# Layer 3 of a four-layer graph network: attention-weight tiles taken in pairs, their products as one run of 64 records

## The chip, the core and the metric

The kernel runs on one core of a Trainium2 chip. The metric is the device time of one execution in microseconds (us), the median of several runs. The core's engines work side by side and meet only at semaphores: TensorE (PE; its weight loads are shown as PEld), VectorE (DVE), ScalarE (ACT), GpSimd (POOL) and SyncE (SP), which here only issues transfers. PE writes its products to PSUM, a small memory of banks of 512 float32 a partition; everything else lives in SBUF.

## The reference: what is computed

Sixteen graphs of 1024 nodes with 256 features pass through four layers; each layer normalises its input (layer norm, then ReLU) and adds its output to it. Layers 0, 1 and 3 are attention layers, layer 2 is a mean over neighbours. Of layer 3, with 4 heads of 64 features, what matters is this:

```python
h = jnp.einsum('bnd,hde->bhne', nodes_embed, W)
e_src = jnp.einsum('bhne,hte->bhtn', h, a_src)
e_dst = jnp.einsum('bhne,hte->bhtn', h, a_dst)
# adjacency is 0 or 1 here, so one edge type is present
weight = mask * (e_src[:, :, 0, :, None] + e_dst[:, :, 0, None, :])
weight = jax.nn.leaky_relu(weight, negative_slope=0.01)
weight = jnp.where(node_adj[:, None] == 0, NEG, weight)
attention = jax.nn.softmax(weight, axis=-1)
dst = jnp.einsum('bhij,bhje->bhie', attention, h) + bias[None, :, None, :]
out = jax.nn.relu(dst) + h          # then a layer norm over the 64 features
```

The exponential of a leaky ReLU of a sum is a maximum of two products, so a tile of unnormalised weights can be made by one DVE instruction from a broadcast row, a column and the mask. The sum of each row of weights comes out of the same product as the result, from a column of its own beside the 64 features: 65 columns a head.

## The kernel before

The sixteen graphs are generators which a small queue steps in turn: a graph starts 120 units of planned time after the one before it, so that about two graphs are under way and one's layer 3 lies beside the next one's layers 0 and 1. The numbers after `yield` are planned time and decide the order in which the program is recorded; a scheduler then fixes the order of each engine. On the chip each engine runs its own list strictly in that order.

The pools that matter: one PSUM pool for layer 3 and layer 2 (`hd_ps`, 2 banks), and three buffers of 128x1024 float32 for the weight tiles of layer 3 (`p3`).

```python
NT, HALF, PER = N // P, 512, 4          # 8 tiles of 128 nodes, 4 of them a PSUM bank
HO, HW = 64, 65
...
hd_ps = ctx.enter_context(tc.tile_pool(name="hd_ps", bufs=2, space=bass.MemoryType.PSUM))
...
def project(norm, w, n, width):         # L659
    ps = mm_ps.tile([P, HALF], F32, tag="mm", name="ps_proj")
    for c in range(DC):
        nc.tensor.matmul(ps[:, :width], norm.ht[:, c, n * P : (n + 1) * P], w[:, c, :width], ...)
    return ps
```

Layer 1 of the next graph, which runs at the same time. The first two output tiles are summed while the weight tiles are still being made, the other six afterwards:

```python
def layer1(b, xs, mask, norm, after):
    ...
    for j in range(NT):
        nc.scalar.activation(hs[:, j, :D], hs[:, j, :D], AF.Copy, scale=hs[:, j, D : D + 1])
        p = weights("p1")                                                    # 8 buffers
        nc.vector.scalar_tensor_tensor(p, row, q[:, j : j + 1], mask[:, j, :], op0=OP.max, op1=OP.mult)  # L793
        ps_.append(p)
        for i, ps in enumerate(early):                                       # two output tiles
            product(ps, i, j)                                                # L786, 128x257
        yield 1.3
    for i in range(NT):
        ...                                                                  # six more, 8 products each
        nc.vector.reciprocal(z, ps[:, D : D + 1])                            # L807
        ...
        residual(xs, i, v, after, e)                                         # L707, L708; then L627
        yield 3.9
```

Layer 3:

```python
def layer3(b, xs, mask, norm, res):
    ...
    yield 8
    for h in range(H):
        next_row = everywhere(d_row[h + 1], "row3") if h + 1 < H else None
        pss = [hd_ps.tile([P, HALF], F32, tag="hd", name="ps_o3") for _ in range(NHALF)]
        for j in range(NT):
            p = work.tile([P, N], F32, tag="p3", name="p3", bufs=3)
            nc.vector.scalar_tensor_tensor(p, row, q[:, j, h : h + 1], mask[:, j, :], op0=OP.max, op1=OP.mult)  # L887

            for i in range(NT):
                g, k = divmod(i, PER)
                for c in range(2):
                    part = slice(c * P // 2, (c + 1) * P // 2)
                    nc.tensor.matmul(                                        # L893
                        pss[g][part, k * HW : (k + 1) * HW], p[:, i * P : (i + 1) * P][:, part], hbv[:, j, h, :],
                        start=(j == 0 and k == 0), stop=(j == NT - 1 and k == PER - 1), skip_group_check=True,
                    )
            yield 1.4
        for g in range(NHALF):
            o = pss[g][:, : PER * HW].rearrange("p (k e) -> p k e", e=HW)
            rz = small.tile([P, PER], F32, tag="rz", name="rz")
            nc.vector.reciprocal(rz, o[:, :, HO])                            # L901
            nc.vector.tensor_tensor(res[:, g * PER : (g + 1) * PER, h, :], o[:, :, :HO], ..., op=OP.mult)  # L902
        row = next_row
    return hs
```

The products of layer 3 use half of the array's columns each: `part` is a slice of 64 columns of weights, so the two products `c = 0` and `c = 1` lie in different halves of the array and write different halves of the partitions. Every float32 product leaves two records in the trace, so a weight tile (8 row tiles x 2 halves) makes 32 records at L893, and a 128-column product of L659 or L786 makes two.

Of the kernel before, what the change touches and what calls it, by code (L numbers as in the profile page):

```python
# [8 lines left out]
F32 = mybir.dt.float32  # L9
U8 = mybir.dt.uint8  # L10
AF = mybir.ActivationFunctionType
OP = mybir.AluOpType
AX = mybir.AxisListType

P = 128
# [406 lines left out]
def tile_simple_stack(  # L422
# [11 lines left out]
    nc = tc.nc  # L434
    B, N, D = x.shape
    NT = N // P
# [5 lines left out]
    PER = NT // NHALF  # L442
# [4 lines left out]
    HW = HO + 1  # L447
# [20 lines left out]
    work = ctx.enter_context(tc.tile_pool(name="work", bufs=2))  # L468
# [187 lines left out]
# [3 lines that stand above are left out]
            nc.tensor.matmul(ps[:, :width], norm.ht[:, c, n * P : (n + 1) * P], w[:, c, :width], start=(c == 0), stop=(c == DC - 1))  # L659
        return ps  # L660

    def new_hs(name="hs"):
        return state.tile([P, NT, W3], F32, tag="hs", name=name, bufs=4)

    def spread(col, n, scales, name):

        k = n * NT  # L670
        ps = tr_ps.tile([P, P], F32, tag="tr", name="ps_col")
        nc.tensor.transpose(ps[:k, :], col, ident)
        all_rows = []
        for scale in scales:
            e = small.tile([H * NT, P], F32, tag="e_row", name="e_row", bufs=2)
            nc.scalar.activation(e[:k, :], ps[:k, :], AF.Exp, scale=scale)
            d = dram.tile([n, N], F32, tag=f"row_{name}", name="d_row", bufs=4)
            later(nc.sync.dma_start(d.rearrange("r (t p) -> (r t) p", p=P), e[:k, :]))
            all_rows += [d[r] for r in range(n)]
        return all_rows  # L680

    def everywhere(d, tag):
        row = work.tile([P, N], F32, tag=tag, name="row", bufs=2)
        later(nc.sync.dma_start(row, d.partition_broadcast(P)))
        return row

    def column(src, n):

        col = small.tile([P, H, NT], F32, tag="col", name="col", bufs=2)
        nc.vector.tensor_copy(col[:, :n, :], src.rearrange("p t n -> p n t"))  # L690
        return col[:, :n, :].rearrange("p n t -> p (n t)")

    def watch(b, layer, terms):
        k = b * 3 + layer
        nc.vector.tensor_reduce(top[:, k : k + 1], terms, axis=AX.XY, op=OP.max, apply_absolute_value=True)
# [163 lines left out]
    def layer3(b, xs, mask, norm, res):  # L859
        hs = new_hs()  # L860
        terms = hs[:, :, D:]
        hb = new_hs("hb")
        hbv = hb[:, :, : H * HW].rearrange("p t (h e) -> p t h e", e=HW)
        for n in range(NT):
            ps = project(norm, wx[3], n, W3)
            nc.scalar.activation(hs[:, n, :], ps[:, :W3], AF.Copy, scale=norm.rs[n])
            if n % 2:
                pair = slice(n - 1, n + 1)
                nc.scalar.activation(hbv[:, pair, :, HO], terms[:, pair, H:], AF.Exp, scale=S3)
                t = hbv[:, pair, :, :HO]  # L870
                hv = hs[:, pair, :D].rearrange("p t (h e) -> p t h e", e=HO)
                bias = rows["bias3"].rearrange("p (h e) -> p h e", e=HO).unsqueeze(1).to_broadcast([P, 2, H, HO])
                nc.vector.tensor_tensor(t, hv, bias, op=OP.add)
                nc.vector.tensor_tensor(t, t, hbv[:, pair, :, HO:].to_broadcast([P, 2, H, HO]), op=OP.mult)
            yield 1.2
        d_row = spread(column(terms[:, :, :H], H), H, (S3 - 1.0,), "l3")
        row = everywhere(d_row[0], "row3")
        watch(b, 2, terms)
        q = small.tile([P, NT, H], F32, tag="q3", name="q3", bufs=2)
        nc.scalar.activation(q, terms[:, :, H:], AF.Exp, scale=1.0 - S3)  # L880
        yield 8
        for h in range(H):
            next_row = everywhere(d_row[h + 1], "row3") if h + 1 < H else None
            pss = [hd_ps.tile([P, HALF], F32, tag="hd", name="ps_o3") for _ in range(NHALF)]
            for j in range(NT):
                p = work.tile([P, N], F32, tag="p3", name="p3", bufs=3)
                nc.vector.scalar_tensor_tensor(p, row, q[:, j, h : h + 1], mask[:, j, :], op0=OP.max, op1=OP.mult)  # L887

                for i in range(NT):
                    g, k = divmod(i, PER)  # L890
                    for c in range(2):
                        part = slice(c * P // 2, (c + 1) * P // 2)
                        nc.tensor.matmul(  # L893
                            pss[g][part, k * HW : (k + 1) * HW], p[:, i * P : (i + 1) * P][:, part], hbv[:, j, h, :],
                            start=(j == 0 and k == 0), stop=(j == NT - 1 and k == PER - 1), skip_group_check=True,
                        )
                yield 1.4
            for g in range(NHALF):
                o = pss[g][:, : PER * HW].rearrange("p (k e) -> p k e", e=HW)
                rz = small.tile([P, PER], F32, tag="rz", name="rz")  # L900
                nc.vector.reciprocal(rz, o[:, :, HO])  # L901
                nc.vector.tensor_tensor(  # L902
                    res[:, g * PER : (g + 1) * PER, h, :], o[:, :, :HO], rz.unsqueeze(2).to_broadcast([P, PER, HO]), op=OP.mult
                )
            row = next_row
        return hs
# [42 lines left out]
    def graph(b):  # L949
        xs = loaded.pop(b)  # L950
        m = masks.pop(b)
        norm = Norm()
        for g in range(NT // 2):
            norm.pair(xs, g)
            m.step()
            yield 2
        for layer, inputs in ((layer0, (m,)), (layer1, (m.bytes,)), (layer2, ())):
            yield 2
            norm.flip()
            after = Norm()  # L960
            yield from layer(b, xs, *inputs, norm, after)
            norm = after
        yield 2
        norm.flip()
        res = state.tile([P, NT, H, HO], F32, tag="res", name="res", bufs=1)
        hs = yield from layer3(b, xs, m.bytes, norm, res)
        return tail(b, xs, hs, res)
# [25 lines left out]
    while queue:  # L993
        queue.sort(key=lambda g: g[:2])
        at, b, g = queue.pop(0)
# [8 lines left out]
    t = work.tile([P, D], F32, tag="e", name="t_bad")[:, : B * NT]  # L1004
# [77 lines left out]
```

## Time and profile before

| | |
|---|---|
| time, median of 3 runs (lowest, highest) | 2709.49 us (2709.22, 2711.38) |
| profiled execution, span | 2701.4 us |
| granted TensorE clock, mean | 0.978 |
| ACT busy | 1432.5 us, 53% |
| PEld busy | 2018.0 us, 75% |
| DMA, mean rate | 87 GB/s |
| seventh graph's layer 3, first weight tile to the next graph's first weight tile | 1205.95 us to 1369.23 us |
| the last graph's layer 3, first weight tile to the last product's start | 2630.14 us to 2673.1 us |

A matmul is recorded with its whole latency, although the next one starts long before it has ended. So a busy PE is not a PE at its peak, and the time a product costs in a stream is the distance between the starts of neighbouring records, not the mean duration. "Idle before" counts only the time in which no record of that engine was open. A wait is put down to the instruction whose semaphore came last. Line numbers are those of the kernel before.

### The profile page before, as it was taken

How to read it: one execution, taken by the hardware profiler on the slowest of the kernel's cores; microseconds unless marked ns; L12 is line 12 of the kernel's file. 1: busy time of each engine (PE TensorE's matmuls, PEld its weight loads, DVE VectorE, ACT ScalarE, POOL GpSimd, SP SyncE). 2: the span in 40 equal slices, each digit the busy share in tenths (PEclk: the TensorE clock that was granted, in tenths of full speed). 3: DMA queues.
4: the chain of work that ended last, by engine and by line, in shares of the span. 5: the costliest groups of instructions: out<-in, count | busy, mean ns of one | idle time of the engine just before them, and what ended most of it. 6: DMA issues, size and time to landing. Idle time of an engine off the chain costs nothing.

```text
span 2701.4 us, 62281 instructions
## 1 busy us (share of the span) xinstructions
PE 2504.5 (93%) x25682; PEld 2018.0 (75%) x25682; DVE 2021.2 (75%) x4069; ACT 1432.5 (53%) x4065; POOL 418.1 (15%) x390
## 2 busy tenths in 40 slices
PE   5899999999999999999999999999999999999985
PEld 4677787776777778687776877778787777877764
DVE  4357768687686977779677687887778777786868
ACT  4663755627455364654637546374653737546250
POOL 1010212102121030211102111020210202121021
PEclk7899999999999999999999999999999999999998
DMA  4431322424223242331413224242332413224121
GB/s 145 117 83 52 114 72 67 122 64 125 76 69 108 65 120 66 98 80 64 133 53 114 72 64 125 65 133 68 96 82 64 133 52 114 74 63 113 37 63 35
DMA packets 146073, 233.73 MB, mean 87 GB/s; under 512 B 9392, under 2 KB 94512, under 8 KB 145776
## 3 DMA queue, kind: packets, MB, share of 16 engines
q1 hardware_dynamic: 74608, 145.73, 16.7%
q0 software_dynamic: 71168, 83.89, 12.4%
q8 instruction: 205, 3.36, 0.5%
q14 instruction: 92, 0.75, 0.1%
HBM read 212.35 MB, written 17.24 MB: 85 GB/s over the span
## 4 chain that ended last, share of the span: by engine, by line
PE 50%; DMA 13%; issue 13%; DVE 13%; ACT 10%; POOL 1%; SPq 0%; DVEq 0%; POOLq 0%; ACTq 0%
PE ps_o L893 14%; PE ps_o L730 12%; PE ps_proj L659 9%; PE ps_o L786 9%; DMA raw<-in_adj_t 5%; PE ps_o L844 5%; DVE p L887 4%; DMA adj<-in_adj 4%; DMA row<-d_row 3%; PE pt_h L653 2%; ACT hn L631 2%; ACT mask L575 2%; ACT unread L635 1%; DMA d_row<-e_row 1%; DVE p L793 1%
## 5 line engine op out<-in xcount | busy, mean ns | idle before, releaser
L887 DVE SCALAR_TENSOR_TENSOR p<-row,q,mask 128x1024 f32<-128x1024 f32 x512 | 635.3, 1276 | 38.8 <-PE ps_o L893 30.0
L659 PE MATMUL ps_proj<-wx,ht 128*128 128x258 f32 (+2 forms) x2048 | 631.5, 444 | 19.4 <-ACT hs L717 12.8
L893 PEld LDWEIGHTS ps_o<-hb,p 128*64 128x64 f32 x16384 | 513.2, 139 | 126.1 <-issue 72.2
L893 PE MATMUL ps_o<-hb,p 128*64 128x65 f32 x16384 | 563.1, 225 | 16.2 <-DVE p L887 11.1
L786 PE MATMUL ps_o<-hs,p 128*128 128x257 f32 x2048 | 529.7, 398 | 50.0 <-DVE p L793 41.0
L730 PE MATMUL ps_o<-hs,p 128*128 128x256 f32 x2048 | 492.6, 387 | 14.5 <-ACT hs L744 14.0
L659 PEld LDWEIGHTS ps_proj<-wx,ht 128*128 128x128 f32 x2048 | 362.2, 190 | 186.7 <-issue 75.5
L786 PEld LDWEIGHTS ps_o<-hs,p 128*128 128x128 f32 x2048 | 372.1, 193 | 112.6 <-issue 48.5
L730 PEld LDWEIGHTS ps_o<-hs,p 128*128 128x128 f32 x2048 | 383.8, 193 | 70.7 <-ACT hs L744 15.3
L592 POOL TENSOR_SCALAR rs<-mv 128x4 f32<-128x4 f32 (+1 forms) x112 | 56.9, 508 | 1600.3 <-ACT unread L635 1584.7
L631 ACT ACTIVATE hn<-xs,shift 128x256 f32<-128x256 f32 x512 | 236.1, 501 | 115.7 <-DVE shift L627 112.9
L707 DVE SCALAR_TENSOR_TENSOR xs<-e,xs 128x256 f32<-128x256 f32 x256 | 108.2, 423 | 236.8 <-ACT e L762 204.3
L593 POOL TENSOR_TENSOR rs<-rs,neg_half 128x4 f32<-128x4 f32 (+2 forms) x144 | 259.7, 1806 | 10.7
L809 ACT ACTIVATE e<-ps_o,shares 128x256 f32<-128x256 f32 x128 | 59.7, 466 | 349.7 <-DVE shares L807 345.5
L575 ACT ACTIVATE mask<-raw 128x512 uint8<-128x512 int32 x256 | 160.5, 630 | 133.8 <-DMA raw<-in_adj_t 114.7
L844 PE MATMUL ps_o<-hi,adj 128*128 128x258 f32 x1024 | 184.9, 308 | 35.5 <-ACT hi L832 23.7
L653 PE MATMUL pt_h<-ident,hn 128*128 128x128 f32 x1024 | 177.5, 283 | 16.5 <-ACT hn L631 16.2
L635 ACT ACTIVATE unread<-xs,shift 128x256 bf16<-128x256 f32 x384 | 190.7, 497 | 0.6
L844 PEld LDWEIGHTS ps_o<-hi,adj 128*128 128x128 f32 x1024 | 144.3, 192 | 60.7 <-ACT hi L832 29.7
L740 DVE SCALAR_TENSOR_TENSOR p<-row,q 128x1024 f32<-128x1024 f32 x128 | 161.1, 1269 | 30.5 <-DMA row<-d_row 30.5
L654 ACT COPY ht<-pt_h 128x512 f32<-128x512 f32 x256 | 147.2, 588 | 67.3 <-PE pt_h L653 66.8
L708 DVE SCALAR_TENSOR_TENSOR xs<-v,xs 128x256 f32<-128x256 f32 x384 | 161.6, 421 | 26.2 <-ACT v L764 9.7
(101 smaller groups left out, 2644.4 us busy)
## 6 DMA issues: line engine op xcount, KB each, us to landing
raw<-in_adj_t SPq DMA_DIRECT2D x256, 256.0 KB
adj<-in_adj POOLq DMA_DIRECT2D x64, 1024.0 KB, 5.8
row<-d_row SPq DMA_DIRECT2D x112, 512.0 KB
xs<-in_x POOLq DMA_DIRECT2D x32, 512.0 KB, 6.3
out<-res SPq DMA_DIRECT2D x32, 512.0 KB
wx<-in_w SPq DMA_DIRECT2D x3, 256.0 KB
d_row<-e_row SPq DMA_DIRECT2D x48, 4.0 KB
wts<-in_w_t SPq DMA_DIRECT2D x2, 256.0 KB
```

Of the source, the lines that this page charges most:

```text
L575: nc.scalar.activation(self.bytes[:, n, g * HALF : (g + 1) * HALF], raw, AF.Square, accum_out=squares[:, k : k + 1])
L593: nc.gpsimd.tensor_tensor(rs[:, :n], rs[:, :n], neg_half[:, :n], op=OP.pow)
L631: nc.scalar.activation(hn, xs[:, 2 * g + k, :], AF.Relu, bias=shift[:, k : k + 1])
L635: nc.scalar.activation(unread, xs[:, 2 * g + k, :], AF.Square, bias=shift[:, k : k + 1], accum_out=self.var[:, 2 * g + k : 2 * g + k + 1])
L653: nc.tensor.transpose(pt[:, c, k * P : (k + 1) * P], hn[:, c * P : (c + 1) * P], ident)
L659: nc.tensor.matmul(ps[:, :width], norm.ht[:, c, n * P : (n + 1) * P], w[:, c, :width], start=(c == 0), stop=(c == DC - 1))
L708: nc.vector.scalar_tensor_tensor(x, v, 0.0, x, op0=OP.max, op1=OP.add, accum_out=after.sums[:, i % 2 : i % 2 + 1])
L730: m = nc.tensor.matmul(ps[:, :D], ps_[j][:, i * P : (i + 1) * P], hs[:, j, :D], start=(j == 0), stop=(j == NT - 1))
L786: nc.tensor.matmul(ps[:, : D + 1], ps_[j][:, i * P : (i + 1) * P], hs[:, j, : D + 1], start=(j == 0), stop=(j == NT - 1))
L844: nc.tensor.matmul(ps[:, : D + 2], adj_n[g][:, i, jj : jj + P], h[:, i, : D + 2], start=(h is hi and i == 0), stop=(h is lo and i == NT - 1),)
L887: nc.vector.scalar_tensor_tensor(p, row, q[:, j, h : h + 1], mask[:, j, :], op0=OP.max, op1=OP.mult)
L893: nc.tensor.matmul(pss[g][part, k * HW : (k + 1) * HW], p[:, i * P : (i + 1) * P][:, part], hbv[:, j, h, :], start=(j == 0 and k == 0), st ...
```

## The change

Layer 3's weight tiles are given out in pairs. The two DVE instructions of a pair come first, then all 32 products of the pair (64 records) as one block. The block starts with the second tile: its products of row tile 0 and row tile 4, one for each bank. So PE waits for the later of the two tiles at the start of the block, and nothing in the block waits for a tile. Then come all products of the first tile, and then the rest of the second. The flags that clear a bank move to the product that is now the first in it. The pool stays at three buffers. The planned time of a step doubles with its content. The purpose is to go less often between products of 64 columns and products of 128 columns.

```diff
-            for j in range(NT):
-                p = work.tile([P, N], F32, tag="p3", name="p3", bufs=3)
-                nc.vector.scalar_tensor_tensor(p, row, q[:, j, h : h + 1], mask[:, j, :], op0=OP.max, op1=OP.mult)
-
-                for i in range(NT):
+            for j in range(0, NT, 2):
+                ps_ = []
+                for jj in range(j, j + 2):
+                    p = work.tile([P, N], F32, tag="p3", name="p3", bufs=3)
+                    nc.vector.scalar_tensor_tensor(p, row, q[:, jj, h : h + 1], mask[:, jj, :], op0=OP.max, op1=OP.mult)
+                    ps_.append(p)
+
+
+                runs = [(1, 0), (1, PER)] + [(0, i) for i in range(NT)] + [(1, i) for i in range(NT) if i % PER]
+                for t, i in runs:
                     g, k = divmod(i, PER)
                     for c in range(2):
                         part = slice(c * P // 2, (c + 1) * P // 2)
                         nc.tensor.matmul(
-                            pss[g][part, k * HW : (k + 1) * HW], p[:, i * P : (i + 1) * P][:, part], hbv[:, j, h, :],
-                            start=(j == 0 and k == 0), stop=(j == NT - 1 and k == PER - 1), skip_group_check=True,
+                            pss[g][part, k * HW : (k + 1) * HW], ps_[t][:, i * P : (i + 1) * P][:, part], hbv[:, j + t, h, :],
+                            start=(j == 0 and t == 1 and k == 0), stop=(j == NT - 2 and t == 1 and k == PER - 1),
+                            skip_group_check=True,
                         )
-                yield 1.4
+                yield 2.8
```

## The prediction

> **What bounds the kernel now.** I read the page's table of engines first, then its groups, then the chain of waits and the timeline of one graph's layer 3. The page:
>
> ```profile
> PE 2504.5 (93%) x25682; PEld 2018.0 (75%) x25682; DVE 2021.2 (75%) x4069; ACT 1432.5 (53%) x4065; POOL 418.1 (15%) x390
> ...
> L887 DVE SCALAR_TENSOR_TENSOR p<-row,q,mask 128x1024 f32<-128x1024 f32 x512 | 635.3, 1276 | 38.8 <-PE ps_o L893 30.0
> ...
> L893 PE MATMUL ps_o<-hb,p 128*64 128x65 f32 x16384 | 563.1, 225 | 16.2 <-DVE p L887 11.1
> L786 PE MATMUL ps_o<-hs,p 128*128 128x257 f32 x2048 | 529.7, 398 | 50.0 <-DVE p L793 41.0
> ```
>
> PE is the bound of the whole, but 93% and 75% are means over stages. The busy time by stretches of the seventh graph (columns: stretch, its length, then PE, PEld, DVE, ACT, POOL) shows which stage the change touches:
>
> ```profile
> 1205.90:1231.00 25.10, 24.33 (x544) 20.43 (x542) 22.74 (x27) 9.84 (x26) 3.18 (x2) 1.00 0.17 56
> 1231.00:1268.00 37.00, 34.77 (x583) 28.14 (x584) 34.48 (x61) 9.13 (x26) 0.00 (x0) 1.00 0.17 57
> 1268.00:1369.00 101.00, 96.02 (x477) 76.69 (x477) 68.45 (x166) 69.46 (x203) 23.78 (x22) 0.98 0.37 107
> ```
>
> In the 62 us that hold layer 3, DVE is busy for 22.74 of 25.1 us and 34.48 of 37: it has as little room as PE. In the 101 us after it, PE is the bound (96.02) and DVE is not. So a gain on PE in layer 3 may be taken by DVE, and a delay there isn't won back later.
>
> What a change between the two kinds of product costs is not an idle time in any view; it stands in the distances of pieces in the chain of waits (start, length, piece):
>
> ```profile
> 1238.68 1.06 PE ps_o L786 x4
> 1239.74 1.08 PE ps_o L893 x32
> 1240.82 1.93 PE ps_o L786 x8
> ...
> 1256.59 2.02 PE ps_o L893 x64
> 1258.60 0.63 PE ps_o L786 x2
> ```
>
> Eight records of 128 columns take 1.93, four take 1.06: 0.217 each, so a visit of four has 0.19 over. 64 records of 64 columns take 2.02, 32 take 1.08: 0.0294 each, so a run has 0.14 over. In the records the three places are plain and alike everywhere: 310 ns instead of 217 before the first record of a run, 152 ns after its last (instead of 52), and 321 instead of 217 between the first two records after it. A round trip costs about 0.32 us.
>
> **What the Trainium skill says.** "TensorEngine Tiling (Array Packing)", section Key Properties: "Changing tiling mode (not just tile) drains the TensorE". Products of 64 columns are column tiles, those of L786 and L659 are not; the 0.32 us is that drain, and the trace agrees that it falls at each change and at no other place. "TensorE: Matmul & The Clock Gate", section Part 3, says that tiles of different columns compute concurrently; the trace agrees: records of a pair start 8 ns apart, and the pairs 60 ns apart. The page gives no price for the drain. I found nothing on the depth of a buffer ring that bears on three buffers taken by twos.
>
> **The change, part by part.** No instruction is added or removed: 512 DVE tiles, 16384 records. The order of PE in the built program changes from 331 runs of 64-column records to 211 (a last run of 1024 is in both). So 120 round trips go, 8 for each of the first 15 graphs: 120 x 0.32 = 38 us of PE, if PE set the time everywhere.
>
> Against it stands the ring of three buffers. Call the tiles of pair k a(k) and b(k), and R(k) the start of its run. Tile n takes the buffer of tile n-3: a(k) that of b(k-2), b(k) that of a(k-1). In the run the last record of a is the 40th, so it starts at R+1.18 (39 x 0.030). Before, DVE started a tile 0.29 after the start of the last record that reads its buffer (1222.56, where the sixteenth record after 1221.82 started at about 1222.27). So b(k) starts no earlier than R(k-1)+1.45; it takes 1.28, and PE starts 0.06 after that (1207.29 after 1205.95+1.28). With nothing else to do, two runs are at least 1.45+1.34 = 2.79 apart, while PE needs 64 x 0.0294 = 1.88 and DVE 2 x 1.20 (8 tiles in 9.64). In the old order the loop was open: three tiles ahead, and DVE ran at 1.20 a tile where PE had room.
>
> I walk the seventh graph in the new order, with these durations, the order of DVE as built, and everything before 1205.95 unchanged. R1 = 1208.84 (b ready; 18 records of L659 stand ahead of it, where 10 did). R2 = 1211.95, R3 = 1215.04, R4 = 1218.13: here PE's own list decides (2.02 + 1.07 for a projection), and DVE waits 0.7 a pair. R5 is the next head: its banks come free when DVE, busy with b(5) until 1220.8, has done the two divisions; 1221.55, PE waits 0.3. Then three runs with only a small transpose between them, each bound by the ring: R6 = 1224.49, R7 = 1227.28, R8 = 1230.07, waits 0.7, 0.9, 0.9. Next L786's first tiles: the old order had DVE make two more layer 3 tiles ahead of them, and PE waited 2.5:
>
> ```profile
> 1225.73 4.89 PE L893 MATMUL ps_o<-hb,p 128*64 128x65 f32 x160
> 1233.14 2.30 PE L786 MATMUL ps_o<-hs,p 128*128 128x257 f32 x8 [2.52 <-DVE p L793]
> ```
>
> In the new order they come right after b(8), at 1229.93, so this wait goes. But it only moves: DVE then has 2 tiles for L793, two divisions and a(9), b(9) in one chain, so R9 = 1235.8 after a wait of 1.6. From here to R12 DVE is busy without a break, and PE waits at the start of each run: R10 = 1240.6 (0.85), R11 = 1246.6 (1.15), R12 = 1250.2 (0.6). R13 = 1254.2, R14 = 1257.7, R15 = 1261.1, R16 = 1264.7 have 0.4 between them. R16 ends at 1266.7, and by then PE has done 6 of the following output tile's L786 records; before, the last run ended at 1267.30 with 16 of them done. Ten records are 2.2, less 0.6: the graph is 1.5 us later. The cross-check: waits of 7.4 instead of 2.9 (2.52 and 0.39), less 8 x 0.32: 1.9. I take 1.5; 15 graphs make 22 us.
>
> The last graph has no other graph beside it, and no round trip to save. Before, DVE ran through it:
>
> ```profile
> 2630.14 12.11 DVE L887 SCALAR_TENSOR_TENSOR p<-row,q,mask 128x1024 f32<-128x1024 f32 x10 [4.32 <-DMA row<-d_row]
> ```
>
> Ten tiles in 12.11; the whole took 43.0 to the last record. New: R1 at 2632.7, 15 steps of 2.79, 0.8 more at each of three changes of head (divisions behind b, then the bank), 2.0 for the last run: 2679.0 instead of 2673.1. It lies at the end of everything: 5.8 us.
>
> Sum: 2709.5 + 22 + 6 = 2737 us, 1% more. Counted by parts: 38 saved in round trips, 38 (15 x 2.5) saved in the wait at L786, and about 104 lost in new waits for the second tile.
>
> **The rivals.**
> (1) PE bound throughout: the 38 us are gained, or more as the wait of L793 (41.0 in all) goes too: 2709 - 38 = 2671, at best 2633. For it: PE's 93%, and that all its waits are only 197 us. Against it: DVE's 92% in this very stretch, so that PE's time can only be saved where DVE hands tiles out sooner, and it doesn't.
> (2) The ring is worse than I walk it: each wait at a run start also holds back the list behind it (L786, then its residual, then the next layer's transposes), so the waits add up through ACT and come back in the 101 us after. DVE's divisions, residuals and tail work are in one list with the tiles. At 3.5 us a graph it would be 2709 + 52 + 6 = 2768. For it: three kinds of work share DVE's list, and the new order of L786 and transposes after the stretch is finer (single products between pairs of transposes). Against it: after the last tile PE has long rows of L786 that wait for nothing.
> (3) Both hardly matter: DVE's total is the same, so the stretch is as long as DVE's work, and the graph ends where it ended: 2709 + 6. For it: DVE idles about 5 us a graph before, and the new waits may fall into those.
>
> **Range and chances.** The walk is a chain of sixteen starts, each good to about 0.1 to 0.2 us, and the scheduler's other shifts are not in it; 1.5 a graph may well be 0 or 3.5. That gives 2737, with 2700 to 2768 for 8 in 10. Rival 1 in full is over 2% only when the L793 wait goes as well and no new one comes: 0.04. Rival 2 must exceed 54 us: 0.2.
>
> **What would show it.** The records between 64- and 128-column products should keep 310, 152 and 321 ns, in 211 runs: else the first term is wrong. L893's line in the groups should show idle time put down to the DVE tile grow from 11.1 us to about 100, and L786's 41.0 nearly vanish. DVE's wait for PE at the tile (30.0) should grow, to some 2 to 3 us a graph. In the last graph runs should start 2.8 us apart. If runs follow each other faster than that with nothing between, the release is earlier than the 40th record plus 0.29 and the prediction is too slow; if the graph's period of 163.3 us doesn't grow, rival 1 or 3 holds.

## The result and the profile after

The changed kernel takes 2726.1 us (median of 4 runs, 2723.6 to 2728.9) against 2709.4 (2705.0 to 2711.4): a ratio of 1.0064, 95% interval 1.0047 to 1.0082, so 13 to 22 us slower. That is within the range of 2700 to 2768, and 11 us under the 2737 that were predicted.

The page of the changed kernel, whose lines L889 and L898 are the former L887 and L893:

```profile
PE 2464.3 (90%) x25682; PEld 2024.5 (74%) x25682; DVE 2022.6 (74%) x4069; ACT 1440.3 (53%) x4065; POOL 391.7 (14%) x390
...
L889 DVE SCALAR_TENSOR_TENSOR p<-row,q,mask 128x1024 f32<-128x1024 f32 x512 | 643.2, 1279 | 53.7 <-PE ps_o L898 44.2
...
L898 PE MATMUL ps_o<-hb,p 128*64 128x65 f32 x16384 | 542.3, 225 | 111.2 <-DVE p L889 103.0
...
L786 PE MATMUL ps_o<-hs,p 128*128 128x257 f32 x2048 | 514.9, 393 | 8.7 <-ACT mask L575 7.7
```

Three things are to be read here. PE's busy time fell from 2504.5 to 2464.3 us, though it has the same 25682 records: busy time contains what the changes between the two kinds of product cost, and 120 round trips went. PE's wait for the tiles of layer 1 (41.0 us at L786) is gone. And PE's wait for layer 3's tiles rose from 11.1 to 103.0, DVE's for their buffers from 30.0 to 44.2. Together PE's idle time went from 197 us (2701.4 - 2504.5) to 263 (2727.1 - 2464.3): 40 saved, 66 lost, 26 between the two profiled executions. Five of these 26 had arisen before the first layer 3: its first weight tile starts at 225.9 us instead of 220.6, and in the profiles of the kernels below that point lies anywhere from 216.9 to 227.7.

The stretches of the seventh graph, from its first weight tile (1217.89) to the end of its layer 3 and on to the next graph's first tile; columns as before (length, then PE, PEld, DVE, ACT, POOL):

```profile
1217.89:1279.50 61.61, 55.30 (x1121) 47.53 (x1120) 57.56 (x86) 17.36 (x46) 2.54 (x2) 1.00 0.16 51
1279.50:1381.45 101.95, 97.00 (x486) 78.22 (x485) 68.20 (x167) 72.30 (x209) 21.96 (x22) 0.98 0.39 111
```

PE idles 6.3 us in the first of them. DVE is busy for 57.56 of 61.61. The whole period, from one graph's first weight tile to the next one's, is 163.56 us, against 163.28 before (1369.23 - 1205.95).

PE's timeline of that stretch, in the middle, where the walk had three runs bound by the buffers and then the alternation with layer 1:

```profile
1236.29 2.09 PE L898 MATMUL ps_o<-hb,p 128*64 128x65 f32 x64 [0.47 <-DVE p L889]
1239.07 2.09 PE L898 MATMUL ps_o<-hb,p 128*64 128x65 f32 x64 [0.69 <-DVE p L889]
1241.84 2.09 PE L898 MATMUL ps_o<-hb,p 128*64 128x65 f32 x64 [0.69 <-DVE p L889]
1243.86 2.00 PE L786 MATMUL ps_o<-hs,p 128*128 128x257 f32 x8
1247.85 2.09 PE L898 MATMUL ps_o<-hb,p 128*64 128x65 f32 x64 [1.99 <-DVE p L889]
1249.86 2.00 PE L786 MATMUL ps_o<-hs,p 128*128 128x257 f32 x8
1252.54 2.09 PE L898 MATMUL ps_o<-hb,p 128*64 128x65 f32 x64 [0.68 <-DVE p L889]
1254.55 2.87 PE L786 MATMUL ps_o<-hs,p 128*128 128x257 f32 x12
1258.52 2.09 PE L898 MATMUL ps_o<-hb,p 128*64 128x65 f32 x64 [1.09 <-DVE p L889]
```

Runs with nothing between them start 2.77 us apart. L786 no longer waits, but every run in these lines does, and all for the second tile of the pair, with which the block starts.

### The profile page after: what moved, and what is told of

It is laid out like the page before. It is cut to its first block, busy times and chain, and to the rows that moved or that the text cites. A ratio compares the mean times of both kernels' runs of the same rounds, so it can differ in the third digit from the quotient of the medians.

```text
span 2727.1 us, 62292 instructions
## 1 busy us (share of the span) xinstructions
PE 2464.3 (90%) x25682; PEld 2024.5 (74%) x25682; DVE 2022.6 (74%) x4069; ACT 1440.3 (53%) x4065; POOL 391.7 (14%) x390
## 4 chain that ended last, share of the span: by engine, by line
PE 35%; DVE 25%; issue 15%; DMA 13%; ACT 11%; POOL 1%; SPq 0%; DVEq 0%; ACTq 0%; POOLq 0%
PE ps_o L730 12%; DVE p L889 9%; PE ps_o L898 7%; PE ps_proj L659 7%; DVE p L793 5%; DMA raw<-in_adj_t 5%; PE ps_o L844 4%; DMA row<-d_row 3%; DMA adj<-in_adj 3%; ACT hn L631 3%; ACT mask L575 3%; PE pt_h L653 2%; PE ps_o L786 2%; DVE xs L708 2%; DMA d_row<-e_row 1%
## 5 line engine op out<-in xcount | busy, mean ns | idle before, releaser
L889 DVE SCALAR_TENSOR_TENSOR p<-row,q,mask 128x1024 f32<-128x1024 f32 x512 | 643.2, 1279 | 53.7 <-PE ps_o L898 44.2
L898 PEld LDWEIGHTS ps_o<-hb,p 128*64 128x64 f32 x16384 | 507.5, 139 | 187.8 <-DVE p L889 118.5
L898 PE MATMUL ps_o<-hb,p 128*64 128x65 f32 x16384 | 542.3, 225 | 111.2 <-DVE p L889 103.0
L659 PE MATMUL ps_proj<-wx,ht 128*128 128x258 f32 (+2 forms) x2048 | 618.8, 442 | 11.4 <-ACT up L835 5.3
L786 PE MATMUL ps_o<-hs,p 128*128 128x257 f32 x2048 | 514.9, 393 | 8.7 <-ACT mask L575 7.7
L659 PEld LDWEIGHTS ps_proj<-wx,ht 128*128 128x128 f32 x2048 | 367.9, 190 | 180.0 <-issue 75.3
L786 PEld LDWEIGHTS ps_o<-hs,p 128*128 128x128 f32 x2048 | 373.6, 193 | 61.0 <-ACT mask L575 7.9
L592 POOL TENSOR_SCALAR rs<-mv 128x4 f32<-128x4 f32 (+1 forms) x112 | 29.4, 263 | 1649.3 <-ACT unread L635 1633.1
L653 PE MATMUL pt_h<-ident,hn 128*128 128x128 f32 x1024 | 179.3, 282 | 30.3 <-ACT hn L631 30.1
L844 PE MATMUL ps_o<-hi,adj 128*128 128x258 f32 x1024 | 178.7, 306 | 28.5 <-ACT hi L832 18.7
L653 PEld LDWEIGHTS pt_h<-ident,hn 128*128 128x128 f32 x1024 | 126.7, 143 | 76.7 <-ACT hn L631 51.2
L844 PEld LDWEIGHTS ps_o<-hi,adj 128*128 128x128 f32 x1024 | 143.0, 192 | 49.5 <-issue 23.6
```

What stands on the lines that cost most here:

```text
L653: nc.tensor.transpose(pt[:, c, k * P : (k + 1) * P], hn[:, c * P : (c + 1) * P], ident)
L786: nc.tensor.matmul(ps[:, : D + 1], ps_[j][:, i * P : (i + 1) * P], hs[:, j, : D + 1], start=(j == 0), stop=(j == NT - 1))
L844: nc.tensor.matmul(ps[:, : D + 2], adj_n[g][:, i, jj : jj + P], h[:, i, : D + 2], start=(h is hi and i == 0), stop=(h is lo and i == NT - 1),)
L889: nc.vector.scalar_tensor_tensor(p, row, q[:, jj, h : h + 1], mask[:, jj, :], op0=OP.max, op1=OP.mult)
L898: nc.tensor.matmul(pss[g][part, k * HW : (k + 1) * HW], ps_[t][:, i * P : (i + 1) * P][:, part], hbv[:, j + t, h, :], start=(j == 0 and t ...
```

## The experiments

Theory R: the loss comes from the ring of three buffers taken by twos, that is, from the place in a run of the record that frees the buffer which the next pair's second tile needs. Rival D: DVE's list is full in this stretch, and a block that needs two finished tiles waits for it whatever the buffers. Rival B: any fourth buffer helps, with the pairs or without.

The table has, for each kernel, the runs of 64-column records in the built program, PE's busy and idle time (span less busy) in the profiled execution, the last graph's layer 3 from its first weight tile to the end of its last product, and the time with its ratio to the kernel before, run beside it on the same chip.

| kernel | runs | PE busy | PE idle | last graph | time | ratio (95%) |
|---|---|---|---|---|---|---|
| before | 331 | 2504.5 | 196.9 | 43.1 | 2709.4 | |
| changed | 211 | 2464.3 | 262.8 | 50.3 | 2726.1 | 1.0064 (1.0047 to 1.0082) |
| e1, room cleared, 3 buffers | 211 | 2463.4 | 265.5 | 49.7 | 2725.6 | 1.0049 (1.0030 to 1.0068) |
| e2, pairs, 4 buffers | 196 | 2468.3 | 220.3 | 45.1 | 2690.7 | 0.9919 (0.9896 to 0.9942) |
| e3, one by one, 4 buffers | 331 | 2509.4 | 197.8 | 43.1 | 2709.8 | 0.9997 (0.9982 to 1.0011) |
| e4, first tile first, 3 buffers | 286 | 2492.9 | 185.0 | 44.0 | 2680.4 | 0.9880 (0.9857 to 0.9903) |
| e5, second tile wholly first | 241 | 2474.7 | 238.5 | 46.9 | 2715.1 | 0.9999 (0.9988 to 1.0010) |
| e6, few tiles, one by one | 296 | 2477.9 | 157.7 | | 2635.5 | 0.9698 (0.9673 to 0.9723) |
| e7, few tiles, pairs | 201 | 2451.7 | 184.5 | | 2625.2 | 0.9664 (0.9641 to 0.9687) |
| e8, first tile first, 4 buffers | 306 | 2478.4 | 176.8 | 42.0 | 2659.0 | 0.9788 (0.9753 to 0.9822) |
| e9, e4 again | 286 | 2491.9 | 180.2 | 43.1 | 2672.9 | 0.9872 (0.9838 to 0.9906) |
| e10, e8 with nothing left out | 306 | 2479.1 | 194.6 | 42.0 | 2688.0 | 0.9920 (0.9892 to 0.9948) |
| e11, e5 with a strict ring | 211 | 2469.2 | 310.0 | 70.2 | 2793.0 | 1.0308 (1.0281 to 1.0336) |

Where an expectation gives 48.2 us for the last graph of the changed kernel, it counts to the start of the last run (2696.71 - 2648.46). The order in which PE works through the whole list changes with nearly every edit, as the column of runs shows. Only in the last graph does PE have nothing else to do, so the ring is seen alone only there.

**e1: the control for the fourth buffer.** SBUF had no room for four buffers. So the bias of layer 2 and the bias, gamma and beta of layer 3 were read from one row (the four parameters are then not the given ones; three of 4069 DVE instructions fall away, the others and their sizes stay), and some small pools were cut. e2, e3 and e8 are cleared in the same way.

```diff
-        for name, src in (("bias2", bias2), ("bias3", bias3), ("gamma3", gamma3), ("beta3", beta3)):
+        for name, src in (("bias3", bias3),):      # and every use of the others reads this row
```

> Control: the changed kernel with the room for a fourth buffer already cleared (layer 2's bias, layer 3's bias, gamma and beta all read one and the same row; a few small pools cut), but still three buffers. The same instructions run. Every theory: 2726 us within 8, 211 runs of 64-column records, PE waiting 103 us for the second tile as before.

Measured: 2725.6 us, the changed kernel's time, and 105.0 us of waits for tiles at L898. No cost and no gain of the clearing shows.

**e2 and e3: the fourth buffer, with the pairs and without.**

```diff
-    tag="p3", name="p3", bufs=3
+    tag="p3", name="p3", bufs=4
```

> The changed kernel, cleared as in e1_slim, with four weight-tile buffers instead of three. Theory R (the ring of three taken by twos makes DVE wait for the run that is under way): the last graph's runs come 2.4 us apart instead of 2.77, DVE's waits for a buffer (44 us) nearly vanish, PE's waits for the second tile fall from 103 us to 50 or less, and the time to 2680 to 2700 us. Rival D (DVE's own list is the bound in this stretch, and a run that needs two tiles before it starts waits for it whatever the buffers): PE's waits stay over 80 us, and the time stays at 2715 to 2726 us.

> The kernel before the change, cleared in the same way, with four buffers. Theory R: a fourth buffer is worth little where tiles go one by one, 0 to 15 us of the 2709, because DVE waited only 30 us for buffers there; 2695 to 2709 us. Rival B (any fourth buffer helps both alike): as much as it helps the pairs, 25 us or more, so 2685 us or less.

Measured: 2690.7 and 2709.8 us. The same buffer is worth 35 us to the pairs (against e1) and nothing to single tiles. PE's groups with pairs and four buffers:

```profile
L898 PE MATMUL ps_o<-hb,p 128*64 128x65 f32 x16384 | 548.9, 226 | 66.1 <-DVE res L908 39.6 <-DVE p L889 24.4
```

The wait for tiles fell from 103.0 to 24.4 us, further than theory R asked, and DVE's wait for a buffer from 44.2 to 13.5. Rival B falls for single tiles. Rival D falls as the whole cause, but it stands in part: PE now waits 39.6 us (7.9 in the changed kernel) for the divisions at a change of head (L908), because there it arrives before DVE has emptied the two PSUM banks. So of the 110.9 us that PE waited for tiles and divisions together, 64.0 are left. In the last graph DVE's timeline shows a head's tiles without a break again, as in the kernel before, and in its last two heads runs start 1.94 to 2.39 us apart:

```profile
2619.92 8.46 DVE L889 SCALAR_TENSOR_TENSOR p<-row,q,mask 128x1024 f32<-128x1024 f32 x7
```

**e4: three buffers, plain order.**

```diff
-                runs = [(1, 0), (1, PER)] + [(0, i) for i in range(NT)] + [(1, i) for i in range(NT) if i % PER]
+                runs = [(t, i) for t in range(2) for i in range(NT)]       # start= moves to t == 0
```

> The changed kernel with three buffers, but the products of a pair in plain order, all of the first tile and then all of the second; the program as built then has 286 runs of 64-column records instead of 211, because other products are put between the two tiles. Theory R: the buffer of the first tile comes free at the 32nd record, not the 40th, and PE needn't wait for the second tile to start, so the last graph is back at 42 to 44 us (from 48.2), and PE's waits at the tiles fall by more than half; but 75 round trips of 0.32 us come back (24 us): 2700 to 2720 us in all. Rival D: the last graph stays over 46 us and the time rises to 2735 us or more.

Measured: 2680.4 us, 1.2% under the kernel before, and better than theory R had it. The last graph is back at 44.0. The lines of PE's waits that matter most:

```profile
PE ps_o L898 <- DVE res L908: 29.5, 17, 1.9
...
PE ps_o L786 <- DVE p L793: 12.6, 16, 7.3
PE ps_o L844 <- DMA adj<-in_adj: 11.6, 16, 1.6
PE ps_o L898 <- DVE p L889: 10.5, 11, 6.1
```

The wait for layer 3's tiles is 10.5 us again, and that for layer 1's is 12.6 instead of 41.0; the wait at changes of head (29.5) was 2.6 in the kernel before and has grown, as in e2. Against the kernel before, PE is busy 11.6 us less (45 round trips fewer) and idle 11.9 less. I had expected the 75 round trips that return to cost 24 us against the changed kernel, and PE's busy time is up by 28.6; what I underrated is how far the waits fall: PE is idle 77.8 us less (262.8 - 185.0).

**e5 and e11: the record that frees the buffer, moved the other way.** All of the second tile, then all of the first:

```diff
-                runs = [(1, 0), (1, PER)] + [(0, i) for i in range(NT)] + [(1, i) for i in range(NT) if i % PER]
+                runs = [(t, i) for t in (1, 0) for i in range(NT)]
```

> The changed kernel with three buffers, but a pair's products in the opposite order: all of the second tile, then all of the first (241 runs as built). The buffer of the first tile then comes free at the 64th record of the run instead of the 40th. Theory R: where nothing lies between, runs are 1.89+0.29+1.34 = 3.5 us apart instead of 2.77, so the last graph takes 56 to 58 us instead of 48.2; the other graphs lose 2 to 4 us each; in all 2760 to 2800 us. Rival D (it is the wait for two finished tiles and DVE's list that cost, not the place of the record that frees the buffer): the last graph stays at 48 us and the time within 10 us of 2726 plus 10 for 30 more round trips.

Measured: 2715.1 us and 46.9 in the last graph. The expectation failed in the wrong direction for theory R, and the time lies under that of rival D too. From the last graph:

```profile
2658.24 2.09 PE L898 MATMUL ps_o<-hb,p 128*64 128x65 f32 x64 [0.46 <-DVE p L889]
2660.79 2.09 PE L898 MATMUL ps_o<-hb,p 128*64 128x65 f32 x64 [0.46 <-DVE p L889]
```

Runs are 2.55 us apart, not 3.5. The built program tells why: the pool doesn't hand out its buffers in turn. It gave the second tile of every pair the same buffer, so b(k) waits for b(k-1), and that is free at the 32nd record of the run, eight records sooner than in the changed kernel. 31 records of 0.030, then 0.29 and 1.34, make 2.56. In the last graph DVE starts the second tile 1.21 us after its run, as the law has it. So the theory had the right law and the wrong buffer.

e5 also shows what the ring does not explain. DVE waits for buffers no longer than in e4 (15.6 us there), yet PE waits for tiles six times as long (10.5 there):

```profile
DVE p L889 <- PE ps_o L898: 15.5, 64, 0.9
PE ps_o L898 <- DVE p L889: 62.7, 93, 7.7
```

The edits differ only in which tile of a pair comes first. The four combinations of order and buffers (e1, e2, e4, e8) say the same: starting with the first tile instead of the second takes 1.7% off the time with three buffers (1.0049 to 0.9880; the last record of the first tile moves from the 40th to the 32nd as well) and 1.3% with four (0.9919 to 0.9788), where in a row of runs no buffer is late (e2). So two things cost here, the late release of a buffer and the start with the tile that is finished last.

To test the law itself, e11 keeps this order of products and hands the three buffers out strictly in turn (three pools of one buffer).

```diff
-    p = work.tile([P, N], F32, tag="p3", name="p3", bufs=3)
+    p = work.tile([P, N], F32, tag=ring(), name="p3", bufs=1)      # ring(): p3_0, p3_1, p3_2 in turn
```

> As e5 (all of the second tile, then all of the first), but the three buffers are handed out strictly in turn, so that the second tile of a pair has to wait for the first tile of the pair before it, whose last record is now the 64th of its run. In e5 the pool gave the second tile of every pair the same buffer, free at the 32nd record. 211 runs as built. Theory R: runs 3.4 to 3.6 us apart in the last graph, which takes 56 to 59 us to its last product; 2 to 4 us lost in each other graph against the changed kernel: 2760 to 2800 us. Rival D: the last graph stays at 45 to 49 us, the time at 2710 to 2730 us.

Measured: 2793.0 us, 3.1% over the kernel before; the last graph takes 70.2. From the first graph's first tile to the last graph's, each graph loses 2.4 us against the changed kernel (2459.2 and 2422.6 us in all), within the 2 to 4. PE's list has 211 runs, as in the changed kernel. From its last graph:

```profile
2706.98 2.09 PE L903 MATMUL ps_o<-hb,p 128*64 128x65 f32 x64 [1.38 <-DVE p L894]
2710.72 2.09 PE L903 MATMUL ps_o<-hb,p 128*64 128x65 f32 x64 [1.65 <-DVE p L894]
2714.45 2.09 PE L903 MATMUL ps_o<-hb,p 128*64 128x65 f32 x64 [1.65 <-DVE p L894]
2719.15 3.32 PE L903 MATMUL ps_o<-hb,p 128*64 128x65 f32 x64 [2.62 <-DVE p L894]
```

The distance is 3.73, where the law gave 3.5. In the built program DVE's list puts the next pair's first tile ahead of this pair's second. It starts at the 32nd record (R+1.20) and ends at R+2.40, past the moment when the 64th record would have let the second tile start (R+1.86+0.29 = R+2.15); 2.40 + 1.34 = 3.74. So it is the 32nd record and two tiles one after the other that set this distance, and a loop bound by the 64th record was not seen. At a change of head it is 4.7. And some runs took 3.2 to 3.5 us instead of 2.09, which no theory had (last section). These three are why the last graph overshot the 56 to 59.

**e6 and e7: the price of a round trip where DVE can't bind.** Only the first two tiles of each head are made, and the rest of the products use them again, so layer 3's result is not computed; the products are all there.

```diff
-                p = work.tile(...)
-                nc.vector.scalar_tensor_tensor(p, row, ...)
+                if j < 2:                                     # e6; in e7 only the first pair of a head
+                    p = work.tile(...)
+                    nc.vector.scalar_tensor_tensor(p, row, ...)
```

> The kernel before the change with most of layer 3's weight tiles left out: only the first two of each head are made, and the second serves for all later products, so the result is not layer 3's. DVE has 384 tiles (460 us) less, and PE doesn't wait for tiles. 296 runs of 64-column records as built. Both theories: 2600 to 2670 us.

> The changed kernel with the same left out: only the first pair of a head is made and serves for all four runs of the head. 201 runs as built, 95 fewer than in e6. Theory R (the gain of fewer round trips is real and was only eaten by the ring): 25 to 40 us less than e6. Rival: if a round trip between the two kinds of product costs nothing when PE is the bound, the two are within 8 us.

Measured: 2635.5 and 2625.2 us, a difference of 10 where 25 to 40 were expected, and the two intervals overlap. PE's busy time shows the price all the same, then its waits in e7:

```profile
PE 2477.9 (94%) x25682; PEld 2012.7 (76%) x25682; DVE 1573.5 (60%) x3685; ACT 1440.7 (55%) x4065; POOL 387.6 (15%) x390
```

```profile
PE 2451.7 (93%) x25682; PEld 2015.7 (76%) x25682; DVE 1565.9 (59%) x3685; ACT 1444.7 (55%) x4065; POOL 384.1 (15%) x390
```

```profile
PE ps_o L898 <- DVE res L908: 24.2, 19, 1.3
```

Busy time fell by 26.2 us for 95 runs fewer, 0.28 each. But PE waits 24.2 us at changes of head for the divisions (in e6 6.6 us), and its idle time is up by 26.8. So in this execution the gain is there and is wholly eaten, for the larger part at the PSUM banks. It is the slowest of e7's five (2638.0 us); in the others less was lost, and where is not known. By the same count of busy time a round trip is worth 0.34 us in the changed kernel (40.2 for 120), 0.33 in e5 (29.8 for 90), 0.27 in e2 (36.2 for 135) and 0.26 in e4 (11.6 for 45), but over 1 us in e8 (26.1 for 25) and e10 (25.4 for 25). The count is rough, because busy time also holds what a lower granted clock adds: that clock was 0.982 and 0.984 in the mean in e8 and e10, and 0.978 in the kernel before. The distances between records (last section) are the better measure.

**e8, e9, e10: is there something better?** Plain order and four buffers, first with the room cleared as in e1, then as a complete kernel; e9 is e4 again beside it.

> The pairs in plain order as in e4, with the fourth buffer (cleared as in e1, so its output is not the reference's). 306 runs as built. Theory R: with the first tile first the ring of three already binds little, so a fourth buffer adds little: 2670 to 2690 us, within 12 of e4's 2680. Rival B (any fourth buffer helps as much as it helped the changed kernel, 35 us): 2650 us or less.

> e4 again, beside e10 on one chip: 2680 us within 8, faster than the kernel before by 1 to 1.4%.

> The pairs in plain order with four buffers, as e8, but with nothing of the computation changed: the room comes from one buffer less for the raw adjacency (two ahead instead of three), one less for the normalised rows (two instead of three), and smaller cuts. Theory R with both prices small: 2655 to 2675 us. Rival: the two smaller pools make ScalarE and the transposes wait (mask for its transfer 104 us before, transposes for ScalarE 13 us in e4), and the fourth buffer's gain is lost: 2680 us or more.

Measured: 2659.0, 2672.9 and 2688.0 us. e8 lies between the two expectations, 21 us under e4. In the profiles the stretch from a graph's first weight tile to the last product of its layer 3 is 56.7 us in the mean instead of 57.4 and the last graph 1.9 us shorter, which makes some 13; its first layer 3 also began 6.4 us earlier, before there was any tile of layer 3. In e10 the room was made with a smaller pool for the raw adjacency and one for the normalised rows:

```diff
-        AHEAD = 3
+        AHEAD = 2
...
-    tag="hn", name="hn", bufs=3
+    tag="hn", name="hn", bufs=2
```

The rival held: the fourth buffer's gain is lost there, and e10 is 15 us slower than e9 beside it. Which of the two pools costs it wasn't separated. The best complete kernel is the pairs in plain order with three buffers: 2680.4 and 2672.9 us in two sets of runs, 1.2 and 1.3% under the kernel before. No part of the computation is left out in it.

## Why the prediction was right, step by step

- **The price and number of round trips** (38 us saved): right. The records at the changes keep 310, 152 and 321 ns, 211 runs stand in the program, and PE's busy time fell by 40.2 us, with the same mean clock of 0.978.
- **The wait of L786 goes** (38 saved): right; 41.0 us went, no wait for L793 is left.
- **The ring's law**, R(k) at least 2.79 after R(k-1) where nothing lies between: measured 2.77 and 2.78. Its terms as written, 1.18 + 0.29, make 1.47 and not 1.45; in the trace the 40th record starts at R+1.16 and the second tile at R+1.44. e2 (four buffers, 1.94 to 2.39), e5 (32nd record and one tile, 2.55) and e11 (32nd record and two tiles, 3.73) show that the freeing record and what DVE does after it set the distance.
- **The walk of the seventh graph**: the first tile starts 11.94 us later than in the kernel before, so R6 to R11 stand at 1224.35, 1227.13, 1229.90, 1235.91, 1240.60 and 1246.58 on the old scale, where the walk had 1224.49, 1227.28, 1230.07, 1235.8, 1240.6 and 1246.6. The last run ended at 1266.35 (1278.29 in its own time) instead of 1266.7, so at equal work the graph is 1.2 us late, not 1.5. By the next graph's first weight tile only 0.3 of that is left (163.56 - 163.28).
- **New waits for the second tile** (about 104 lost): the wait at L898 for tiles rose by 91.9.
- **The last graph** (5.8): 7.2 (50.3 - 43.1). Its first two runs, after a wait of 7.31 us, took 6.61 us together instead of 2.09 each, at a granted clock of 0.59, and so stand 3.82 and 3.57 us before the next; the walk had 2.79 there. In the kernel before, too, the first 256 records of the last graph took 9.59 us and the next 256 took 8.56, so this explains only a part.
- **The term that was mis-sized is the 22 us of the fifteen graphs.** From the first graph's first tile to the last graph's first tile it is 2422.6 us instead of 2409.5 (2648.46 - 225.85 and 2630.14 - 220.61): 13 us, 0.87 a graph in the mean, with single periods from 1.1 us shorter to 3.0 longer. 0.3 of the missing 0.6 is the end of the walk; where the rest is made good was not followed. 13 + 7 = 20 agrees with the 13 to 22 of the interval; the 5 us before the first layer 3 make up the 26 of the two profiles.
- **Rival 2** (waits come back downstream) was true in small: the transposes' wait for ScalarE rose from 16.2 to 30.1 us, while other waits fell by some 13 (L659's for ScalarE's copy at L717 from 12.8 to 5.0, L844's for L832 from 23.7 to 18.7), and L844's for DVE at L836 rose from 1.1 to 9.1.
- **Rival 3** (the graphs end where they ended, 2715 us) was half right: of the 1.5 us a graph that the prediction set against it, 0.87 came.
- **Rival 1** was right about PE and wrong about the rest. What the prediction didn't see is how little stood between the two: with the plain order of the same pairs (e4) most of the waits don't arise, and the kernel is faster by more than the changed one is slower.

One sentence of the prediction was true only by luck: that tile n takes the buffer of tile n-3. Within a graph of the changed kernel it does; in e5 it doesn't, and there the buffers are handed out in the order in which they are released.

## What to carry to other kernels

When work is grouped to save a switch, follow the buffers before the switch: find the record in the group that frees the buffer which the next group's last input needs, and add producer time, release and start; if that loop is longer than both engines' own time, the grouping makes a wait that wasn't there. A group that starts with its latest input keeps its inside free of waits, but it shifts the release of the other input back and hides nothing of the producer's time. Here, letting the group start on the first tile kept 45 of the 120 saved switches and brought PE's wait for tiles back to 10.5 us, where a fourth buffer alone left 24.4 and 39.6 at the changes of head.

## What the runs showed of the hardware

- A change between products of 64 and of 128 columns and back costs 0.30 us of PE's time (93 + 100 + 104 ns). No wait and no idle time shows it. It is paid in three places, in the median the same to 1 or 2 ns in the kernel before, the changed one, e6 and e7: 93 ns before the first 64-column record, 100 after the last, 104 between the first two 128-column records.
- In e11's last graph PE's granted clock fell though no gap near it was longer than 2.62 us. Over the run at 2702.19, after a gap of 2.61 us, and over that at 2719.15, the answers by stretch read (granted clock third from the end):

```profile
2702.00:2706.90 4.90, 3.41 (x64) 3.25 (x64) 2.59 (x3) 0.00 (x0) 0.00 (x0) 0.65 0.00 0
2707.00:2718.00 11.00, 6.24 (x192) 5.82 (x192) 7.31 (x10) 0.00 (x0) 0.00 (x0) 1.00 0.14 51
2719.00:2723.00 4.00, 3.32 (x64) 3.16 (x64) 1.78 (x3) 0.00 (x0) 0.00 (x0) 0.58 0.00 0
```

The run of 64 records took 3.3 to 3.4 us there instead of 2.09, and so released its buffers later. In this kernel waits of that length thus cost twice. In the changed kernel's last graph the runs from the third on, with gaps of 0.7 to 1.3 us, kept 2.08 to 2.19. A threshold doesn't come out of these runs: in e2's last graph the clock fell to 0.50 after a gap of 2.05 us, but stayed at 1.00 after one of 2.14.
